# State's part of y in a Mamba and FP4 block: one 64-row float32r contraction for a 16-row float32 one

## The chip, the cores and the metric

The kernel runs on one core of one Trainium2 chip. The metric is the device time of one execution in microseconds, as the median of several runs. The engines have short names in the profile: PE is TensorE (PEld its weight loads), DVE is VectorE, ACT is ScalarE, POOL is GpSimd and SP is SyncE, which here only issues DMA transfers.

## What is computed

One layer of a simplified Mamba block on 8 sequences of 2048 tokens, followed by a gated feed-forward part whose operands are rounded to FP4 by blocks of 16. Everything is float32. Cut to what matters here:

```python
D_MODEL, D_STATE, D_CONV, D_INNER = (256, 16, 4, 512)
xz = x @ W_in
x_proj, z = jnp.split(xz, 2, axis=-1)
x_conv = silu((conv(x_proj) + conv_b))
ssm = x_conv @ W_xproj
delta = jax.nn.softplus(ssm[..., 0])
Bm = ssm[..., 1:1 + D_STATE]
Cm = ssm[..., 1 + D_STATE:]
deltaB = delta[..., None] * Bm
h_mean = jnp.einsum('bld,bln->bdn', x_conv, deltaB) / L
y = jnp.einsum('bdn,bln->bld', h_mean, Cm)
y = y + D[None, None, :] * x_conv
y = y * silu(z)
return y @ W_out
```

`h_mean` is a mean over all tokens of a sequence, so `y` of a sequence's first token needs its last one. The contraction that this case is about is the second einsum: for each token, 512 channels out of 16 states.

## The kernel before

The tokens are worked through in 32 blocks of 512 (four blocks to a sequence), and the second half of the work in pairs of 128-token tiles (two pairs to a block). The program is a list of small pieces. Each piece is entered by `at` with a due time from a hand-written table (`BLOCK` and `PAIR` in the middle, `FIRST`, `BEGIN`, `END`, `FINAL`, `LAST` at the ends, all in us on a plan of 64 us a block), the list is sorted by due time, and the pieces are issued in that order. Every engine runs its own instructions strictly in that order and waits on semaphores for its operands. So a due time sets no clock time: it sets what stands ahead of what in each engine's queue, the SP's DMA queue included.

A block's first part (`begin_block`) loads x transposed, projects it (L756), convolves it (`first` L770 and `tap` L776 on ACT and DVE), applies silu, and then `x_projection` (L802) gives Bm and Cm: one PSUM tile of 128 partitions, four groups of 32 rows, one group to each of four sets of 128 tokens; in a group the first 16 rows are Cm and the last 16 are Bm. `keep_ssm` (L812, ACT) copies it to SBUF as `ct`, in the pool `keep` with six buffers, since Cm is used four blocks later (`LAG` = 4); `by_token` (L817, DVE) transposes it. `weigh` and `softplus` (L651 to L675, with one POOL step `sp_e`, L654) give delta, and `sums` (L896) adds up the state over a sequence in one PSUM bank.

At a sequence's last block, `mean` (L906, ACT) scales that sum, `spread_mean` (L910, TensorE) multiplies it with `spread`, a matrix of ones and zeros that adds the four groups' parts and puts the same result into all four groups of 32 rows, and `keep_mean` (L916, ACT) copies it to SBUF as `hT` (states by channels).

`mix_block` comes four blocks later. `state` (L966) forms y for the block: for each of four chunks of 128 channels and each of four token sets t, a product over the 16 rows of group t, into one of four PSUM banks:

```python
g = slice(t * G, t * G + DS)
nc.tensor.matmul(s["y"][t][:, c, :], hT_of[b][g, c * P : (c + 1) * P], s["ct"][g, :], ...)
```

`mix` (L977, DVE) adds each bank to the skip part in SBUF. `finish_pair` then gates it with silu(z) (`gated`, L1031, POOL), multiplies with W_out (`out`, L1038), normalizes, rounds to FP4, and does the gate, up (L1061) and down products (`tails` L1094 and `down` L1105).

The rounding has a detour that matters here (`quantize_turned`): block scales are turned on DVE (L518), written to DRAM by four small transfers (`gather_scales`, `q_rows`, L524), read back repeated over partitions (`spread_scales`, L531, into `xqT` or `hqT`), while the rounded values are transposed by DMA (`turn`, L538, `q_gT`); POOL multiplies the two (L541). All these transfers, the loads of x (L739, L1004 for `xTz`, L1008 for `xt`), the transposes `hwT` (L841) and the stores (L1118) are issued on SP's one queue. PSUM has seven banks in the pool `ps` for all products and one for the state sum.

Of the kernel before, what the change touches and what calls it, by code (L numbers as in the profile page):

```python
# [8 lines left out]
F32 = mybir.dt.float32  # L9
BF16 = mybir.dt.bfloat16  # L10
U16 = mybir.dt.uint16
AF = mybir.ActivationFunctionType
ALU = mybir.AluOpType
AX = mybir.AxisListType
PSUM = bass.MemoryType.PSUM

P = 128
# [23 lines left out]
    "x_projection": 91.66,  # L41
    "keep_ssm": 94.60,
    "by_token": 99.56,
    "negate": 94.19,
    "exp": 95.71,
    "ratio": 104.25,
# [6 lines left out]
    "mean": 127.54,  # L53
    "spread_mean": 127.90,
    "keep_mean": 129.60,
    "state": 70.83,
    "mix": (79.04, 76.36, 71.79, 75.27),
    "weigh": (90.45, 90.69, 90.49, 92.15),
# [54 lines left out]
    "x_projection": 93.30,  # L113
    "keep_ssm": 109.81,
    "by_token": 112.25,
    "negate": 96.50,
    "exp": 106.60,
    "ratio": 107.91,
# [6 lines left out]
    "mean": 126.28,  # L125
    "spread_mean": 129.37,
    "keep_mean": 130.82,
    "state": 72.50,
    "mix": (74.93, 78.14, 76.66, 78.28),
    "weigh": (85.52, 89.72, 94.26, 90.27),  # L130
# [145 lines left out]
def mamba_fp4_ffn_kernel(  # L276
# [16 lines left out]
    nc = tc.nc  # L293
    B, L, DM = x.shape
    DI = w_out.shape[0]
    DS = (w_xproj.shape[1] - 1) // 2
# [5 lines left out]
    TT = T // P  # L302
# [7 lines left out]
    G = 32  # L310
# [6 lines left out]
    const = ctx.enter_context(tc.tile_pool(name="const", bufs=1))  # L317
    ps = ctx.enter_context(tc.tile_pool(name="ps", bufs=7, space=PSUM))
    ps_h = ctx.enter_context(tc.tile_pool(name="ps_h", bufs=1, space=PSUM))
    dram = ctx.enter_context(tc.tile_pool(name="dram", bufs=2, space=bass.MemoryType.DRAM))  # L320

    ident = const.tile([P, P], F32, name="ident")
# [29 lines left out]
    for dB in dB_of:  # L352
        nc.gpsimd.memset(dB, 0.0)

    place = const.tile([P, G], F32, name="place")
    nc.vector.tensor_reduce(place, ident.rearrange("p (j n) -> p n j", n=G), AX.X, ALU.add)
    spread = const.tile([P, TT, G], F32, name="spread")
    nc.vector.tensor_copy(spread, place.unsqueeze(1).to_broadcast([P, TT, G]))

    xpool = ctx.enter_context(tc.tile_pool(name="xpool", bufs=2))  # L360
    keep = ctx.enter_context(tc.tile_pool(name="keep", bufs=LAG + 2))
    p2 = ctx.enter_context(tc.tile_pool(name="p2", bufs=2))
# [36 lines left out]
    def at(base, table, name, index, f, *args):  # L399
        place = table[name]  # L400
        for i in index:
            place = place[i]
        events.append((base + place, len(events), f, args))

    def bank():
        return ps.tile([P, 512], F32, tag="ps", name="ps")
# [4 lines left out]
    def round_fp4(at_piece, v, n, homes=None, turned=None):  # L411
# [56 lines left out]
        def magnify():  # L468
            nc.scalar.activation(state["g"], state["x"], AF.Abs, scale=GRID)  # L469

# [213 lines left out]
    def layernorm(at_piece, r, nt=NT):  # L684
# [22 lines left out]
        def apply(t):  # L707
            nc.scalar.activation(  # L708
                r()[:, t, :],
                r()[:, t, :],  # L710
                AF.Identity,
                bias=v["nb"][:, t : t + 1],
# [9 lines left out]
    hsum_of, hs_of, hT_of = {}, {}, {}  # L722

    def begin_block(n):
# [5 lines left out]
        b, i = divmod(n, NBLK)  # L730
        early = n < NBLK
        s = tiles["block", n] = {}

        def at_piece(name, f, *args):
            at(n * PERIOD, FIRST if early else BLOCK, name, args, f, *args)
# [31 lines left out]
        def first(c):  # L767
            if "xc" not in s:
                s["xc"] = keep.tile([P, NC, T], F32, tag="xc", name="xc")
            nc.scalar.activation(  # L770
                s["xc"][:, c, :], s["xp", c][:, 0:T], AF.Copy, scale=cw_sb[:, c, 0:1]
            )
# [18 lines left out]
        def silu(c):  # L791
            if "xc" not in s:
                s["xc"] = keep.tile([P, NC, T], F32, tag="xc", name="xc")
            acc = s["xc"][:, c, :]
            nc.scalar.activation(acc, s.pop(("mm", c), acc), AF.Silu, bias=cb_sb[:, c : c + 1])

# [11 lines left out]
                    )  # L808

        def keep_ssm():  # L810
            s["ct"] = keep.tile([P, P], F32, tag="ct", name="ct")
            nc.scalar.copy(s["ct"], s.pop("mm"))  # L812

        def by_token():

# [16 lines left out]
        def split(c):  # L832

            s["hw", c] = p2.tile([P, 2, T], U16, tag="hw", name="hw")
            nc.scalar.copy(
                s["hw", c], s["xc"][:, c, :].bitcast(U16).rearrange("p (n h) -> p h n", h=2)
            )

        def turn(c):
            s["hwT", c] = p2.tile([P, 2, TT, P], U16, tag="hwT", name="hwT")  # L840
            nc.sync.dma_start_transpose(  # L841
                s["hwT", c].rearrange("p h t n -> p (h t) n"),
                s.pop(("hw", c)).rearrange("p h n -> p (h n)"),
            )

        def turned(c):
            if "xct" not in s:
                s["xct"] = p2.tile([P, TT, DI], F32, tag="xct", name="xct", bufs=1)
            nc.scalar.copy(
                s["xct"][:, :, c * P : (c + 1) * P]  # L850
                .bitcast(U16)
                .rearrange("p t (n h) -> p t n h", h=2),
# [51 lines left out]
        def mean():  # L904
            hs = hs_of[b] = p2.tile([P, DI], F32, tag="hs", name="hs", bufs=1)
            nc.scalar.activation(hs, hsum_of.pop(b), AF.Copy, scale=1.0 / L)  # L906

# [4 lines left out]
            )  # L912

        def keep_mean():
            hT_of[b] = p2.tile([P, DI], F32, tag="hT", name="hT", bufs=1)
            nc.scalar.copy(hT_of[b], hs_of.pop("mm"))  # L916

        def skip(c):
            nc.scalar.activation(
                s["xc"][:, c, :], s["xc"][:, c, :], AF.Copy, scale=dk_sb[:, c : c + 1]  # L920
            )

        at_piece("load", load)
        for c in range(NC):
# [10 lines left out]
            at_piece("skip", skip, c)  # L935
        at_piece("x_projection", x_projection)
        at_piece("keep_ssm", keep_ssm)
        at_piece("by_token", by_token)
        for t in range(TT if early else 0):
            at_piece("turn", turn_early, t)  # L940
            at_piece("turned", turned_early, t)
# [9 lines left out]
        if i == NBLK - 1:  # L951
            at_piece("mean", mean)
            at_piece("spread_mean", spread_mean)
            at_piece("keep_mean", keep_mean)

    def mix_block(n):

        b = n // NBLK
        s = tiles["block", n]

        def state():
            s["y"] = [bank().rearrange("p (c n) -> p c n", n=P) for _ in range(TT)]
            for c in range(NC):
                for t in range(TT):
                    g = slice(t * G, t * G + DS)
                    nc.tensor.matmul(  # L966
                        s["y"][t][:, c, :],
                        hT_of[b][g, c * P : (c + 1) * P],
                        s["ct"][g, :],
                        start=True,  # L970
                        stop=True,
                    )

        def mix(g):
            xc = s["xc"].rearrange("p c (t g r) -> p g c t r", g=TT, r=G)[:, g]
            y = s["y"][g].rearrange("p c (t r) -> p c t r", r=G)
            nc.vector.tensor_tensor(xc, xc, y, ALU.add)  # L977

        table = FIRST if n < NBLK else FINAL if n == B * NBLK - 1 else BLOCK
        at((n + LAG) * PERIOD, table, "state", (), state)  # L980
        for t in range(TT):
            at((n + LAG) * PERIOD, table, "mix", (t,), mix, t)
# [312 lines left out]
    for n in range(B * NBLK):  # L1295
        begin_block(n)
        mix_block(n)
        for half in range(T // U):
            finish_pair(n * (T // U) + half)
# [58 lines left out]
```

## Time and profile before

| | |
|---|---|
| Three runs | 1780.77, 1781.19, 1781.21 us (median 1781.19) |
| Span of the profiled execution, first to last instruction | 1781.8 us |
| Granted TensorE clock, mean | 0.995 |
| TensorE busy, 0 to 100 us / 100 to 300 / 300 to 1500 / 1500 to 1782 | 86.2 / 199.0 / 1199.8 / 269.1 us |
| DVE busy in the same four stretches | 77.2 / 182.9 / 1111.8 / 228.1 us |
| State contraction, L966 | 1024 records of matmul, 1024 of weight load |
| DMA packets, and what they moved | 367467, 199.41 MB |

A float32 product is two records in the profile, each with its own weight load. Busy time counts from the first to the last record of overlapping ones; a matmul's end is modelled. The chain that ended last is followed back from the last instruction; in it a group's time runs from its start to the start of what follows. In the lists of groups the columns are: line, engine, operation, output<-inputs, shape, count | busy us, mean ns of one | idle us of the engine before them, and what ended most of it. In a timeline: start us, length us, engine, line, operation, and in brackets the idle time before it and what released it. SPq is SP's DMA queue.

### The profile page before, as it was taken

To read this page: it belongs to the slowest core of one execution; us is meant where nothing else is said; L and a number is where in the kernel's file an instruction comes from. 1 tells how busy PE (TensorE), PEld (TensorE's weight loads), DVE (VectorE), ACT (ScalarE), POOL (GpSimd) and SP (SyncE) were. 2 spreads that over 40 slices of the span, in tenths; PEclk is the share of its full clock that TensorE was granted. 3 is DMA by queue.
4 is the path that set the end of the run, shared out by engine and by line. 5 is a ranking of instruction groups with operands and counts; after the bars stand their busy time and mean duration, and the time that the engine had idled before them with its cause. 6 is when DMAs were issued, how large, how long until landed. Compare 5 with 4: busy or idle time off the path is not lost.

```text
span 1781.8 us, 27851 instructions
## 1 busy us (share of the span) xinstructions
PE 1754.2 (98%) x9646; PEld 1385.7 (78%) x9646; DVE 1600.0 (90%) x3138; ACT 998.7 (56%) x1534; POOL 775.3 (44%) x966
## 2 busy tenths in 40 slices
PE   7999999999999999999999999999999999999997
PEld 3567787787787787787777787777787778888885
DVE  6998999999999999999999989989999989987876
ACT  5786566655566655565655566655566655532232
POOL 2233454444445344444444444344444444544553
PEclk9999999999999999999999999999999999999998
DMA  3234555555556545556544565554555554544432
GB/s 108 71 86 105 125 131 117 113 107 117 120 122 133 114 96 116 122 125 126 116 104 111 122 126 123 116 107 111 122 126 117 121 103 108 117 104 105 113 79 68
DMA packets 367467, 199.41 MB, mean 112 GB/s; under 512 B 290272, under 2 KB 342368, under 8 KB 367328
## 3 DMA queue, kind: packets, MB, share of 16 engines
q1 hardware_dynamic: 367328, 197.65, 49.9%
q8 instruction: 76, 1.25, 0.3%
q14 instruction: 63, 0.52, 0.1%
HBM read 116.34 MB, written 20.91 MB: 77 GB/s over the span
## 4 chain that ended last, share of the span: by engine, by line
PE 94%; DVE 4%; issue 1%; POOL 0%; ACT 0%; DMA 0%; SPq 0%; ACTq 0%; POOLq 0%; DVEq 0%
PE ps L1061 33%; PE ps L1105 15%; PE ps L1015 13%; PE ps L1038 12%; PE ps L756 12%; PE ps L1094 2%; PE ps L966 2%; PE ps L802 2%; PE hsum L896 2%; DVE xc L776 1%; DVE q_amax L438 0%; PE ps L910 0%; PE ps L865 0%; DVE xd L882 0%; DVE q_w L477 0%
## 5 line engine op out<-in xcount | busy, mean ns | idle before, releaser
L1061 PE MATMUL ps<-wgT,xqT 128*128 128x256 f32 (+1 forms) x1512 | 324.4, 361 | 0.0
L1061 PE MATMUL ps<-wuT,xqT 128*128 128x256 f32 (+1 forms) x1512 | 319.6, 361 | 0.0
L1061 PEld LDWEIGHTS ps<-wgT,xqT 128*128 128x128 f32 x1512 | 276.7, 190 | 40.8 <-issue 12.7
L1061 PEld LDWEIGHTS ps<-wuT,xqT 128*128 128x128 f32 x1512 | 275.6, 190 | 38.4 <-issue 12.2
L776 DVE SCALAR_TENSOR_TENSOR xc<-xp,cw_sb,xc 128x512 f32<-128x512 f32 x372 | 282.1, 780 | 13.5 <-DMA dk_sb<-in_L_attn_D_dram 6.3
L541 POOL TENSOR_TENSOR hqT<-q_gT,hqT 128x1408 f32<-128x1408 bf16 x63 | 188.9, 2998 | 230.1 <-DMA q_gT<-q_w 213.9
L1105 PE MATMUL ps<-wdT,hqT 128*128 128x256 f32 x1260 | 288.8, 384 | 0.0
L1079 ACT ACTIVATE sg<-ps 128x512 f32<-128x512 f32 (+1 forms) x189 | 105.4, 558 | 308.4 <-PE ps L1061 260.6
L1031 POOL TENSOR_TENSOR xc<-xc,sz 128x512 f32<-128x512 f32 x128 | 168.5, 1337 | 249.7 <-DVE xc L977 215.7
L1105 PEld LDWEIGHTS ps<-wdT,hqT 128*128 128x128 f32 x1260 | 234.2, 190 | 44.3 <-issue 11.6
L756 PE MATMUL ps<-xT,w_in_sb 128*128 128x512 f32 x512 | 242.1, 598 | 7.0 <-DMA xT<-in_x_t_dram 7.0
L1015 PE MATMUL ps<-xTz,w_in_sb 128*128 128x256 f32 x1024 | 244.3, 382 | 0.0
L1015 PEld LDWEIGHTS ps<-xTz,w_in_sb 128*128 128x128 f32 x1024 | 191.3, 190 | 58.8 <-issue 14.0
L1038 PE MATMUL ps<-w_out_sb,xc 128*128 128x256 f32 x1008 | 228.3, 379 | 0.9 <-POOL xc L1031 0.9
L1038 PEld LDWEIGHTS ps<-w_out_sb,xc 128*128 128x128 f32 x1008 | 190.4, 190 | 37.2 <-issue 11.2
L1026 ACT ACTIVATE sz<-ps 128x512 f32<-128x512 f32 x128 | 75.8, 593 | 245.8 <-PE ps L1015 245.8
L477 DVE SCALAR_TENSOR_TENSOR q_w<-q_w,q_x 128x512 bf16<-128x512 bf16 (+3 forms) x131 | 184.0, 1404 | 2.3
L541 POOL TENSOR_TENSOR xqT<-q_gT,xqT 128x512 f32<-128x512 bf16 x63 | 77.8, 1235 | 228.4 <-DMA xqT<-q_rows 105.8
L708 ACT ACTIVATE x<-x,ln_nb,ln_rs 128x256 f32<-128x256 f32 x256 | 142.3, 591 | 50.2 <-POOL ln_nb L705 42.1
L473 DVE SCALAR_TENSOR_TENSOR q_x<-q_w,q_x 128x512 f32<-128x512 bf16 (+3 forms) x131 | 155.6, 1188 | 14.0 <-ACT q_w L469 13.9
L1086 DVE TENSOR_TENSOR h<-sg,ps 128x512 f32<-128x512 f32 (+1 forms) x189 | 115.3, 631 | 52.8 <-PE ps L1061 48.0
L756 PEld LDWEIGHTS ps<-xT,w_in_sb 128*128 128x128 f32 x512 | 96.4, 192 | 79.7 <-issue 74.8
(128 smaller groups left out, 2440.1 us busy)
## 6 DMA issues: line engine op xcount, KB each, us to landing
hqT<-q_rows SPq DMA_DIRECT2D x63, 704.0 KB
xT<-in_x_t_dram SPq DMA_DIRECT2D x32, 512.0 KB
xTz<-in_x_t_dram SPq DMA_DIRECT2D x64, 256.0 KB
xt<-in_L_attn_x_dram SPq DMA_DIRECT2D x64, 256.0 KB
xqT<-q_rows SPq DMA_DIRECT2D x63, 256.0 KB
out_dram<-x SPq DMA_DIRECT2D x63, 256.0 KB
q_rows<-q_scT SPq DMA_DIRECT2D x252, 4.0 KB
q_rows<-q_scT SPq DMA_DIRECT2D x252, 12.0 KB
```

The lines of the kernel that those rows point to most:

```text
L473: nc.vector.scalar_tensor_tensor(xn, w, 1.5 * GRID, xn, ALU.max, ALU.subtract)
L477: nc.vector.scalar_tensor_tensor(w, w, 1.5 * GRID, xn, ALU.max, ALU.subtract)
L541: nc.gpsimd.tensor_tensor(qT(), state["gT"], qT(), ALU.mult)
L708: nc.scalar.activation(r()[:, t, :], r()[:, t, :], AF.Identity, bias=v["nb"][:, t : t + 1], scale=v["rstd"][:, t : t + 1],)
L756: nc.tensor.matmul(mm, w_in_sb[:, k, c * P : (c + 1) * P], s["xT"][:, k, :], start=(k == 0), stop=(k == KM - 1),)
L776: nc.vector.scalar_tensor_tensor(acc, xp[:, k + 1 : k + 1 + T], cw_sb[:, c, k + 1 : k + 2], acc, ALU.mult, ALU.add)
L1015: nc.tensor.matmul(q["mm", j][:, a, :], w_in_sb[:, k, DI + c * P : DI + (c + 1) * P], q["xT"][:, k, :], start=(k == 0), stop=(k == KM - 1),)
L1031: nc.gpsimd.tensor_tensor(xc, xc, q["sz"][:, c, :], ALU.mult)
L1038: nc.tensor.matmul(mm[:, t, :], s["xc"][:, c, o : o + P], w_out_sb[:, c, :], start=(c == 0), stop=(c == NC - 1),)
L1061: nc.tensor.matmul(q[name, j][:, t, :n], q["xqT"][:, t * KM + k, :], wT[:, k, f0 : f0 + n], start=(k == 0), stop=(k == KM - 1),)
L1086: nc.vector.tensor_tensor(h, q.pop(("sg", j)), up, ALU.mult)
L1105: nc.tensor.matmul(q["d"][t], q["hqT"][:, t * (NF + 1) + j, :], wdT[t][:, t + j, :], start=False, stop=(j == NF - 1),)
```

## The change

The result of `x_projection` is taken apart into a float32r value (`high`, what remains when it is written as float32r) and the exact rest (`low`); the same is done with the state. All four products of the parts then stand under each other on 64 partitions, in one float32r contraction. `cs` has, for each half of 64 partitions (two token sets, side by side in its second dimension), 32 rows of the high part of Cm and 32 of the low part, each twice 16 rows; `hT` alternates high and low by 16 rows. `cs` is made by a detour through DRAM: one write of both parts (`put_parts`) and eight reads (`get_parts`) of 16 partitions each. `hT` is made in two steps: ACT writes the float32r copy, and DVE then forms copy x (0 or -1) + value, so that rows 16 to 31 of each group become the rest. `spread` now repeats the state every 16 rows.

```diff
+    "high": 95.50,
+    "low": 99.60,
+    "put_parts": 101.0,
+    "get_parts": 113.0,
...
+    "part_mean": 129.61,
...
-    place = const.tile([P, G], F32, name="place")
-    nc.vector.tensor_reduce(place, ident.rearrange("p (j n) -> p n j", n=G), AX.X, ALU.add)
-    spread = const.tile([P, TT, G], F32, name="spread")
-    nc.vector.tensor_copy(spread, place.unsqueeze(1).to_broadcast([P, TT, G]))
+    place = const.tile([P, DS], F32, name="place")
+    nc.vector.tensor_reduce(place, ident.rearrange("p (j n) -> p n j", n=DS), AX.X, ALU.add)
+    spread = const.tile([P, P // DS, DS], F32, name="spread")
+    nc.vector.tensor_copy(spread, place.unsqueeze(1).to_broadcast([P, P // DS, DS]))
+
+    low_rows = const.tile([P, 1], F32, name="low_rows")
+    nc.vector.tensor_reduce(
+        low_rows, ident.rearrange("p (j n) -> p n j", n=G)[:, DS:, :], AX.XY, ALU.add
+    )
+    nc.vector.tensor_scalar(low_rows, low_rows, -1.0, None, ALU.mult)
...
         def keep_ssm():
-            s["ct"] = keep.tile([P, P], F32, tag="ct", name="ct")
-            nc.scalar.copy(s["ct"], s.pop("mm"))
+            s["ct"] = p2.tile([P, P], F32, tag="ct", name="ct")
+            nc.scalar.copy(s["ct"], s["mm"])
+
+        def high():
+            s["hl"] = p2.tile([P, 2, P], F32, tag="hl", name="hl")
+            nc.scalar.copy(s["hl"][:, 0, :].bitcast(F32R), s.pop("mm"))
+
+        def low():
+            nc.gpsimd.tensor_tensor(s["hl"][:, 1, :], s["ct"], s["hl"][:, 0, :], ALU.subtract)
+
+        def put_parts():
+            s["parts"] = dram.tile([2, P, P], F32, tag="parts", name="parts")
+            nc.sync.dma_start(s["parts"].rearrange("h p t -> p h t"), s.pop("hl"))
+
+        def get_parts():
+            s["cs"] = keep.tile([P, 2, P], F32, tag="cs", name="cs")
+            for half in range(2):
+                for h in range(2):
+                    o = (half * 2 + h) * G
+                    rows = s["parts"][h].rearrange("(g r) t -> r g t", r=G)
+                    rows = rows[:DS, 2 * half : 2 * half + 2, :]
+                    for rep in range(2):
+                        nc.sync.dma_start(s["cs"][o + rep * DS : o + (rep + 1) * DS], rows)
...
         def keep_mean():
+            hs_of["high"] = p2.tile([P, DI], F32, tag="hs", name="h_high", bufs=1)
+            nc.scalar.copy(hs_of["high"].bitcast(F32R), hs_of["mm"])
+
+        def part_mean():
             hT_of[b] = p2.tile([P, DI], F32, tag="hT", name="hT", bufs=1)
-            nc.scalar.copy(hT_of[b], hs_of.pop("mm"))
+            nc.vector.scalar_tensor_tensor(
+                hT_of[b].bitcast(F32R),
+                hs_of.pop("high"),
+                low_rows,
+                hs_of.pop("mm"),
+                ALU.mult,
+                ALU.add,
+            )
...
             for c in range(NC):
-                for t in range(TT):
-                    g = slice(t * G, t * G + DS)
-                    nc.tensor.matmul(
-                        s["y"][t][:, c, :],
-                        hT_of[b][g, c * P : (c + 1) * P],
-                        s["ct"][g, :],
-                        start=True,
-                        stop=True,
-                    )
+                for j in range(2):
+                    for half in range(2):
+                        g = slice(half * 2 * G, (half + 1) * 2 * G)
+                        nc.tensor.matmul(
+                            s["y"][2 * half + j][:, c, :],
+                            hT_of[b][g, c * P : (c + 1) * P].bitcast(F32R),
+                            s["cs"][g, j, :].bitcast(F32R),
+                            start=True,
+                            stop=True,
+                        )
...
-    nc = _bacc.Bacc("TRN2", target_bir_lowering=False, num_devices=1)
+    nc = _bacc.Bacc(
+        "TRN2", target_bir_lowering=False, num_devices=1, dynamic_dma_scratch_size=1024
+    )
```

All other due times are as they were. In the order that results, on each engine: ACT does `high` right after `keep_ssm`; POOL does `low` after `sp_e` and the gating of a half (two L1031) in an ordinary block; SP has `put_parts` between an `xTz` load and the four `q_rows` transfers, and the eight `get_parts` after the next `xTz` load, just ahead of a `q_gT` transpose; DVE has `part_mean` ahead of some of the convolution's taps.

More of the change, by code (lines that the diff above doesn't have):

```diff
@@ L11 @@
 U16 = mybir.dt.uint16
+F32R = mybir.dt.float32r
 AF = mybir.ActivationFunctionType
@@ L115 @@
     "by_token": 112.25,
+    "high": 109.83,
+    "low": 112.00,
+    "put_parts": 113.0,
+    "get_parts": 123.0,
     "negate": 96.50,
@@ L127 @@
     "keep_mean": 130.82,
+    "part_mean": 130.83,
     "state": 72.50,
@@ L938, in begin_block @@
         at_piece("by_token", by_token)
+        at_piece("high", high)
+        at_piece("low", low)
+        at_piece("put_parts", put_parts)
+        at_piece("get_parts", get_parts)
         for t in range(TT if early else 0):
@@ L954, in begin_block @@
             at_piece("keep_mean", keep_mean)
+            at_piece("part_mean", part_mean)
     def mix_block(n):
```

## Prediction

> **What bounds the kernel now.** I read the busy shares first, then the chain that ended last, then the groups of the state contraction kept apart by shape, then timelines around one batch end and one ordinary block.
>
> ```profile
> PE 1754.2 (98%) x9646; PEld 1385.7 (78%) x9646; DVE 1600.0 (90%) x3138; ACT 998.7 (56%) x1534; POOL 775.3 (44%) x966
> PE 94%; DVE 4%; issue 1%; POOL 0%; ACT 0%; DMA 0%; SPq 0%; ACTq 0%; POOLq 0%; DVEq 0%
> ```
>
> TensorE is the bound: between 300 and 1500 us it is busy for 1199.8 of 1200 us. A microsecond taken from it comes off the end, and one for which it must wait is added. The state contraction and its nearest relatives:
>
> ```profile
> L966 PE MATMUL ps<-ct,hT 16*128 16x128 f32 x1024 | 37.5, 283 | 0.3
> L966 PEld LDWEIGHTS ps<-ct,hT 16*128 16x128 f32 x1024 | 31.4, 186 | 11.3 <-DVE xc L776 3.6 <-ACT hT L916 3.4 <-issue 3.3
> L802 PEld LDWEIGHTS ps<-xc,w_xp_sb 128*32 128x32 f32 x1024 | 26.3, 110 | 11.2 <-issue 7.1 <-DVE xd L882 2.0 <-DVE xc L776 1.0
> L865 PEld LDWEIGHTS ps<-ident,xc 128*128 128x128 f32 x64 | 8.3, 155 | 5.9 <-ACT xc L795 4.6 <-issue 1.3
> ```
>
> One block's state is 16 products in 32 records. In the chain of waits it takes 1.10 us (1.17 where it waited for hT first):
>
> ```profile
> 704.18 0.86 PE ps L910 x2
> 705.03 0.63 PE ps L1094 x4
> 705.71 1.17 PE ps L966 x32
> 729.52 1.01 PE ps L802 x32
> ```
>
> Here a batch ends: spread_mean (L910), a tails group, then state, which starts 0.05 us after hT's copy (705.07 + 0.59) ends. In all eight batches state waits for that copy.
>
> ```profile
> 703.92 4.41 DVE L776 SCALAR_TENSOR_TENSOR xc<-xp,cw_sb,xc 128x512 f32<-128x512 f32 x6
> 705.07 0.59 ACT L916 COPY hT<-ps 128x512 f32<-128x512 f32 x1 [1.22 <-PE ps L910]
> ```
>
> The SP queue of one block, and what it feeds on POOL and TensorE:
>
> ```profile
> 731.01 1.76 SPq L524 DMA_DIRECT2D q_rows<-q_scT  x4
> 734.04 0.62 SPq L531 DMA_DIRECT2D hqT<-q_rows  x1
> 745.89 1.42 SPq L538 DMA_TRANSPOSE q_gT<-q_w  x1
> 735.73 2.50 POOL L1031 TENSOR_TENSOR xc<-xc,sz 128x512 f32<-128x512 f32 x2
> 749.57 2.89 POOL L541 TENSOR_TENSOR hqT<-q_gT,hqT 128x1408 f32<-128x1408 bf16 x1 [6.07 <-DMA q_gT<-q_w]
> 758.44 0.63 PE ps L1094 x4
> ```
>
> hqT is scaled by 752.46, and the tails that read it start at 758.44: six microseconds to spare.
>
> **The contraction itself: -1.6 us.** The build of the changed program has 9134 matmul records where the page shows 9646: 16 fewer in each of 32 blocks, so a product is one record, not two. Four row tiles with 8 records each become two row tiles with 8 each. [...] The weight loads do not fall: loads of 32 columns take 110 ns, of 128 columns 186, whatever the rows; 76 ns for 96 columns, so 101 ns for 128, and eight in a row tile are 0.81 us. [...] I take 1.05, the row with the same load.
>
> [...]
>
> **The wait at a batch's end: +6.1.** hT now needs a copy on ACT (high, as before) and then part_mean on DVE. DVE operations of 128x512 take 0.63 (three mixes in 1.88) to 0.78 us (L776); I take 0.70, plus 0.06 for one more hand-over: 0.76, eight times. Nothing covers it, since state waits for that copy today. It stands in DVE's order behind the two ln_mv pairs of the boundary, at 703.92 in the block shown, so DVE waits there for the copy until 705.67, and the six taps and the mixes behind come 2.4 us later. DVE idles 2.22 us at 717.5 for a product's L1061, which takes most of that up.
>
> **In the first batch the taps behind it are on the path: +2.4.** There DVE does seven taps from 91.70 to 96.92 and mixes at 97.73; POOL gates at 100.36 and TensorE takes L1038 at 101.68 with idle time ahead of it. Now two taps end at 93.2, part_mean runs 96.5 to 97.2, five taps (0.745 each) end at 100.9, and the mixes start 3.2 later, 0.76 of it counted already.
>
> **The detour through DRAM: +8.4.** Each block adds a copy on ACT (0.25 like ct's 0.27; ACT then idles 5.96 us), a subtraction on POOL (128x512 takes 1.25: 0.31, with fixed cost 0.35) and nine transfers on SP at 0.42 to 0.47. None of these is on TensorE's chain; were the covers gone they would cost 8, 11 and 120 us. But they stand in queues. POOL does low after the gated pair, at 738.2 to 738.6. put_parts waits for it and stands before q_rows, which today issue at 731.01. In the changed order's waits there is a second thing: SP's transfers take eight completion semaphores in turn, and the seventh get has the one of hqT, so it waits until hqT (704 KB; its last packet ends 7.2 us after the issue's end, median of 63) has landed; q_gT stands behind. From low: put 0.47, q_rows 1.76, landing 1.27 (732.77 to 734.04), hqT 0.62 + 7.2, two gets 0.85, q_gT 1.42, its landing 2.26 (747.31 to 749.57), POOL 2.89: 18.8 us. In this block 738.6 + 18.8 = 757.4 against 758.4: 1.0 left of six. I did that sum for blocks 6 to 31: twelve have 0.8 to 1.3 left, twelve 1.8 to 3.8, and the last two are late: low at 1487.7 against tails at 1505.65 (0.85 late) and 1536.6 against 1552.93 (2.5 late). That is +3.4. The first pair has the same with xqT: put at 116.6, q_rows to 118.9, xqT 120.1 to 120.8, xTz and eight gets to 124.6, q_gT 3.1 later than its 121.49, and L1061 at 125.5 has 0.1 in hand: +3.0. For inner blocks in which DVE's lateness at a batch end eats the last microsecond I take +2.0 (2.4 late, of which 1.0 to 1.4 is covered, in some two of seven batch ends). Bounds of the chain: 2 us shorter leaves only +1.0 (part of the first pair); 2 us longer puts TensorE about 1 us late in twelve blocks and 2 more in each of the last two, +16. The extra traffic, 0.25 MB in each block or 8 MB to 199 MB, runs beside it.
>
> [...] Row first: L1105 with 20 records takes 4.51 us after a tiled group against 20 x 0.2156 = 4.31. [...]
>
> **Sum:** -1.6 + 6.1 + 2.4 + 8.4 = +15.3. The profiled span is 1781.8, 0.6 above the median of 1781.19; from the median, 1796.5. I say 1797.
>
> **Rivals.**
> [...]
> *The detour is longer*: hqT shares its engines with 16 KB gets and a late xTz, one more microsecond or two, and twelve blocks stall: 1796.5 + 16 - 2 (the inner blocks' share, in it already) = 1811. For: slack of 1.0 in half of the blocks. Against: DMA was idle from 743 to 746.
> [...]
>
> **Chances.** The sum with its own bounds (1789 to 1804, the fourth case in it) 0.52; longer detour 0.22; dearer product 0.06; loads that do not bind 0.20, in it 0.08 faster by over 0.2%, 0.05 within, 0.07 slower. 0.2%, 3.6 us, is about what a measurement here can tell from no change. So faster 0.08, same 0.05, slower 0.87. Range: from 1784, where the third of the fast cases begins, to 1819, which takes in the longer detour and leaves the dearer product out.
>
> **What would show it.** State at 1.05 in the chain with 16 loads still at 186 ns; below 0.80 my first term is wrong. TensorE idle about 0.8 us before each of eight states with DVE as releaser. q_gT issued some 4 us later in a block, POOL's hqT ending within 1.5 us of the tails, and TensorE waiting for POOL's hqT at the tails of the last two blocks; if inner blocks wait too, the detour was under-sized. An unchanged idle table with a shorter state would make the whole forecast wrong.

## The result, and the profile after

The changed kernel takes 1858.22 us (median of 1845.06 to 1860.20) against 1781.20: a ratio of 1.041, with an interval of 1.0376 to 1.0443. The forecast was 1797 with a range from 1784 to 1819; slower was right, the size was not: +77 us instead of +15.3. The profiled execution has a span of 1857.4 us, 75.6 more than before.

From the page of the changed kernel, the busy times and the chain that ended last:

```profile
PE 1775.8 (96%) x9134; PEld 1399.0 (75%) x9134; DVE 1626.5 (88%) x3148; ACT 1006.2 (54%) x1566; POOL 826.8 (45%) x998
PE 65%; DVE 23%; DMA 5%; issue 4%; POOL 1%; ACT 1%; SPq 1%; DVEq 0%; ACTq 0%; POOLq 0%
```

TensorE was 94% of the chain and is 65% now; DVE went from 4% to 23%, DMA from 0 to 5%. TensorE's busy time grew by 21.6 us, so 54.0 of the 75.6 us are idle time: 31.1 of them lie between 300 and 1500 us, where before it idled 0.2. The busy time grew although the contraction has fewer records, because ahead of TensorE's last product the granted clock stood at half for 58.0 us in 13 stretches, against 13.7 us in 3 before. At the batch end shown below, 3.4 us of half clock cost down 1.69 us (6.20 against 4.51), half of them; at that rate it is at most 22.2 us more.

The change moved the lines: the gate and up products L1061 are now L1118, tails L1151 (before L1094), down L1162 (L1105), residual1 L1105 (L1048), POOL's scaling L558 (L541), the normalization of 1408 elements on DVE L478 (L461). The kernels of the experiments differ from that by a few lines again.

The groups of the new operations (the columns are those of before):

```profile
L1023 PE MATMUL ps<-cs,hT 64*128 64x128 f32 x512 | 40.7, 301 | 15.3 <-issue 10.4 <-DVE hT L960 4.9
L1023 PEld LDWEIGHTS ps<-cs,hT 64*128 64x128 f32 x512 | 36.2, 203 | 20.4 <-issue 18.3 <-PE ps L653 1.1
L960 DVE SCALAR_TENSOR_TENSOR hT<-h_high,low_rows,ps 128x512 fp32r<-128x512 f32 x8 | 5.8, 720 | 2.2 <-ACT h_high L956 2.2
```

There are 512 records instead of 1024, as forecast, and part_mean takes 0.72 us (forecast 0.70). The mean of 203 ns a load includes stretches at half clock. But the state's records had 11.3 us of idle time ahead of their loads before and have 20.4 now. The batch end that the prediction showed now stands at 732 in the chain:

```profile
732.19 0.86 PE ps L950 x2
733.05 0.63 PE ps L1151 x4
733.68 2.07 issue
735.75 1.11 PE ps L1023 x16
736.86 6.20 PE ps L1162 x20
743.06 4.75 PE ps L1118 x24
```

State waits 2.07 us, not 0.76, since part_mean starts only at 734.94, behind work for which DVE is itself late. And down (L1162, 20 records) takes 6.20 us instead of 4.51. TensorE by stretches there (busy, granted clock, DMA share, GB/s) tells why:

```profile
735.70:737.20 1.50, 1.45 (x18) 1.00 0.63 120
737.20:739.20 2.00, 2.00 (x7) 0.55 0.27 51
739.20:741.20 2.00, 2.00 (x7) 0.59 0.57 108
741.20:743.20 2.00, 2.00 (x11) 1.00 0.75 189
```

After the idle time the clock is granted at half for 3.4 us.

What makes DVE late shows in the list of waits (engine, line, what was waited for: us in total, times, longest):

```profile
POOL hqT L558 <- DMA q_gT<-q_w: 328.7, 30, 13.8
DVE x L1105 <- DMA out_dram<-x: 68.6, 24, 4.7
PE ps L1118 <- DVE xc L1034: 14.9, 15, 1.5
PE ps L1151 <- POOL hqT L558: 14.7, 10, 3.8
```

The second line has no counterpart before: residual1 (L1105) waits for a store. Here is the SP queue of the next block, and what the eight gets wait for in all blocks:

```profile
769.94 0.36 SPq L842 DMA_DIRECT2D parts<-hl  x1
770.40 1.83 SPq L541 DMA_DIRECT2D q_rows<-q_scT  x4
773.79 0.62 SPq L548 DMA_DIRECT2D hqT<-q_rows  x1
775.04 8.88 SPq L852 DMA_DIRECT2D cs<-parts  x8
784.02 1.43 SPq L555 DMA_TRANSPOSE q_gT<-q_w  x1
785.55 0.71 SPq L1175 DMA_DIRECT2D out_dram<-x  x1
SPq L852 <- DMA hqT<-q_rows: 125.5, 26, 5.2
```

The eight gets take 8.88 us, because the seventh waits for hqT's semaphore; that and their place ahead of q_gT were foreseen. Behind q_gT, though, stands the store, at 785.55. It sends x1 out, of which there are four buffers, and residual1 of a later pair has to wait until its buffer has been sent. Before, the store was issued 5.9 us ahead of residual1:

```profile
748.07 0.38 SPq L1118 DMA_DIRECT2D out_dram<-x  x1
753.94 0.63 DVE L1048 TENSOR_TENSOR x<-xt,ps 128x512 f32<-128x512 f32 x1
754.48 1.61 DVE L461 TENSOR_TENSOR q_x<-h,q_rs 128x1408 f32<-128x1408 f32 x1
```

Here is what DVE and POOL do now:

```profile
787.72 2.88 POOL L558 TENSOR_TENSOR hqT<-q_gT,hqT 128x1408 f32<-128x1408 bf16 x1 [12.34 <-DMA q_gT<-q_w]
788.22 0.69 DVE L1105 TENSOR_TENSOR x<-xt,ps 128x512 f32<-128x512 f32 x1 [3.12 <-DMA out_dram<-x]
788.82 3.26 DVE L478 TENSOR_TENSOR q_x<-h,q_rs 128x1408 f32<-128x1408 f32 x1
790.65 0.70 PE L1151 MATMUL ps<-wdT,hqT 64*128 64x256 f32 x4 [0.55 <-POOL hqT L558]
```

DVE idles 3.12 us until the store has landed. By then POOL has started the scaling of hqT, since q_gT, issued just ahead of the store, has landed too. And the next DVE operation, L478, takes 3.26 us where it takes 1.62 alone: it ends 1.48 us after POOL's. Its groups, before and now:

```profile
L461 DVE TENSOR_TENSOR q_x<-h,q_rs 128x1408 f32<-128x1408 f32 x63 | 105.9, 1680 | 0.0
L478 DVE TENSOR_TENSOR q_x<-h,q_rs 128x1408 f32<-128x1408 f32 x63 | 156.0, 2476 | 0.0
```

That is 50 us more in all. In 25 of 63 pairs it takes over 3 us, each time under POOL's scaling of hqT, which makes 40 us; most of the rest is in 14 pairs in which it starts under the shorter scaling of xqT and takes 2.4 to 2.6. The tails (L1151) wait only 0.55 us for POOL: what the prediction watched is a small part of it.

### The profile page after: what moved, and what is told of

It is laid out like the page before. It is cut to its first block, busy times and chain, and to the rows that moved or that the text cites. A ratio compares the mean times of both kernels' runs of the same rounds, so it can differ in the third digit from the quotient of the medians.

```text
span 1857.4 us, 27357 instructions
## 1 busy us (share of the span) xinstructions
PE 1775.8 (96%) x9134; PEld 1399.0 (75%) x9134; DVE 1626.5 (88%) x3148; ACT 1006.2 (54%) x1566; POOL 826.8 (45%) x998
## 4 chain that ended last, share of the span: by engine, by line
PE 65%; DVE 23%; DMA 5%; issue 4%; POOL 1%; ACT 1%; SPq 1%; DVEq 0%; ACTq 0%; POOLq 0%
PE ps L1118 26%; PE ps L1162 11%; PE ps L773 8%; PE ps L1095 8%; PE ps L1072 7%; DVE xc L793 6%; DVE q_x L478 4%; DMA out_dram<-x 3%; DVE q_amax L455 2%; DVE h L1143 2%; PE ps L1151 1%; PE ps L819 1%; DVE ln_st L711 1%; DVE q_x L490 1%; DVE q_w L494 1%
## 5 line engine op out<-in xcount | busy, mean ns | idle before, releaser
L1118 PE MATMUL ps<-wgT,xqT 128*128 128x256 f32 (+1 forms) x1512 | 328.6, 363 | 14.9 <-DVE xc L1034 14.9
L558 POOL TENSOR_TENSOR hqT<-q_gT,hqT 128x1408 f32<-128x1408 bf16 x63 | 181.8, 2886 | 358.1 <-DMA q_gT<-q_w 328.7
L1118 PE MATMUL ps<-wuT,xqT 128*128 128x256 f32 (+1 forms) x1512 | 323.5, 364 | 3.4 <-POOL xqT L558 3.4
L1118 PEld LDWEIGHTS ps<-wgT,xqT 128*128 128x128 f32 x1512 | 275.4, 190 | 61.1 <-DVE xc L1034 21.5
L1118 PEld LDWEIGHTS ps<-wuT,xqT 128*128 128x128 f32 x1512 | 275.3, 191 | 46.1 <-issue 12.2
L1162 PE MATMUL ps<-wdT,hqT 128*128 128x256 f32 x1260 | 305.0, 400 | 0.0
L793 DVE SCALAR_TENSOR_TENSOR xc<-xp,cw_sb,xc 128x512 f32<-128x512 f32 x372 | 289.9, 801 | 11.1 <-ACT xc L787 7.8
L1162 PEld LDWEIGHTS ps<-wdT,hqT 128*128 128x128 f32 x1260 | 245.8, 199 | 47.8 <-issue 11.6
L486 ACT ACTIVATE q_w<-q_x 128x512 bf16<-128x512 f32 (+3 forms) x131 | 130.3, 994 | 83.8 <-DVE q_x L478 79.7
L490 DVE SCALAR_TENSOR_TENSOR q_x<-q_w,q_x 128x512 f32<-128x512 bf16 (+3 forms) x131 | 149.9, 1144 | 11.6 <-ACT q_w L486 11.2
L478 DVE TENSOR_TENSOR q_x<-h,q_rs 128x1408 f32<-128x1408 f32 x63 | 156.0, 2476 | 0.0
L889 ACT COPY xct<-hwT 128x1024 uint16<-128x1024 uint16 x112 | 129.1, 1160 | 44.5 <-DMA hwT<-hw 43.8
```

Of the source, the lines that this page charges most:

```text
L478: nc.vector.tensor_tensor(x, by_block(v()), rs.unsqueeze(len(rs.shape)).to_broadcast(x.shape), ALU.mult,)
L490: nc.vector.scalar_tensor_tensor(xn, w, 1.5 * GRID, xn, ALU.max, ALU.subtract)
L558: nc.gpsimd.tensor_tensor(qT(), state["gT"], qT(), ALU.mult)
L793: nc.vector.scalar_tensor_tensor(acc, xp[:, k + 1 : k + 1 + T], cw_sb[:, c, k + 1 : k + 2], acc, ALU.mult, ALU.add)
L1118: nc.tensor.matmul(q[name, j][:, t, :n], q["xqT"][:, t * KM + k, :], wT[:, k, f0 : f0 + n], start=(k == 0), stop=(k == KM - 1),)
L1162: nc.tensor.matmul(q["d"][t], q["hqT"][:, t * (NF + 1) + j, :], wdT[t][:, t + j, :], start=False, stop=(j == NF - 1),)
```

## Experiments

**The change in its three parts.** Each of the first three kernels keeps the contraction and leaves out the detour, part_mean or both; the fourth is complete and moves the detour.

`a1_contraction`: the contraction alone.

```diff
-                            s["cs"][g, j, :].bitcast(F32R),
+                            cs_fixed[g, j, :].bitcast(F32R),
...
-        at_piece("high", high)
-        at_piece("low", low)
-        at_piece("put_parts", put_parts)
-        at_piece("get_parts", get_parts)
...
-            nc.scalar.copy(hs_of["high"].bitcast(F32R), hs_of["mm"])
+            nc.scalar.copy(hT_of[b].bitcast(F32R), hs_of.pop("mm"))
...
-            at_piece("part_mean", part_mean)
```

> The float32r contraction alone: neither the detour nor part_mean; the state reads a fixed tile of zeros in place of C's parts, and hT is the plain copy, so State's part of y is left out. As forecast (loads bind, nothing else changes): state 1.05, -1.6 us, 1779.6. Other theory, from the changed kernel's trace, where the time from the first tails record to the record behind state is 1.475 us against 1.736 before (tails and state now follow each other 0.28 us closer, state itself 0.02 longer): 28 blocks x 0.26 and three x 0.06, -7.5, 1773.7.

Measured 1776.45 us (1776.05 to 1776.67), ratio 0.9969 (0.9957 to 0.9982): -4.75. The chain of this kernel:

```profile
756.33 0.63 PE ps L1148 x4
756.96 0.84 PE ps L1020 x16
757.80 4.51 PE ps L1159 x20
```

and its loads:

```profile
L1020 PEld LDWEIGHTS ps<-cs_fixed,hT 64*128 64x128 f32 x512 | 32.8, 188 | 5.3 <-ACT hT L958 3.4 <-issue 1.0
```

A float32r load takes 188 ns, as a float32 one does (186). Tails and state together take 1.47 us, against 0.63 + 1.10 = 1.73. By the records' starts the 0.26 lie at the seam: the first state record stands 0.35 us behind the first of the tails, where it stood 0.63 behind, and state itself is no shorter.

`a2_mean`: the contraction and part_mean; of the edits above, those on `cs` and the detour alone.

> The contraction with part_mean on DVE, without the detour (State reads the fixed zeros, its part of y is left out). As forecast for the wait at batch ends and the first taps: +6.1 and +2.4 on top of the contraction alone, so 1782 if that is 1773.7. Rival (the wait and the halved clock behind it are part_mean's own doing): at seven batch ends the changed kernel's trace has 1.4 to 3.6 us more ahead of L1162 and 1.7 lost to a granted clock of 0.5: about 4 us eight times, 1805. If the detour makes DVE late and so the wait long, there is no clock of 0.5 at batch ends here.

Measured 1791.23 us (1786.01 to 1792.13), ratio 1.0044 (1.0028 to 1.0060), 14.8 above the contraction alone; the profiled execution was the shortest, 9.5 above. A batch end in its chain:

```profile
707.52 0.87 PE ps L952 x2
708.42 0.59 ACT h_high L958
709.04 0.76 DVE hT L962
709.93 1.11 PE ps L1021 x16
711.04 4.51 PE ps L1160 x20
```

This is the wait as forecast: TensorE idles 0.92 us at six batch ends and 2.38 at the last, and down stays at 4.51. The 2 us waits of the changed kernel are not part_mean's own. The other executions, some 5 us longer, had a mean granted clock of 0.993 instead of 0.998; they have no trace. In the traced one none of TensorE's idle times of 2.4 to 2.9 us past 100 us was followed by a half clock; whether some were in the others is not shown.

`a3_detour`: the contraction and the detour; of the edits above, those on the mean alone.

> The contraction with the detour, without part_mean: hT is the plain rounded copy, so the low half of the state's mean is left out. As forecast: +8.4 on top of the contraction alone, 1782 if that is 1773.7. Theory now (put and gets at their place on SP hold q_gT and the store behind them, so hqT and x1's buffers are late in every block): most of the 85 us between 1773.7 and 1858 is here, 1825 to 1850. Rival (part_mean's wait and the clock are the larger part): under 1805.

Measured 1833.25 us (1828.64 to 1839.01), ratio 1.0287 (1.0264 to 1.0310), 56.8 above the contraction alone. From its list of waits:

```profile
DVE x L1104 <- DMA out_dram<-x: 67.2, 27, 4.1
```

So the wait for the store needs no part_mean. The parts give 14.8 + 56.8; together they cost 81.8 more than the contraction alone, 10 more than their sum.

`a4_later`: complete.

```diff
-    "put_parts": 101.0,
-    "get_parts": 113.0,
+    "put_parts": 110.0,
+    "get_parts": 121.5,
```

> Complete; only two due times differ from the changed kernel: put_parts from 101 to 110 (behind the scales' gathers and hqT's issue), get_parts from 113 to 121.5 (behind q_gT and the store). If the place on SP is what costs: near the contraction with part_mean alone, 1780 to 1790, q_gT issued some 4 us earlier in the block than in the changed kernel and no wait of DVE's residual1 for the store above 1 us. If the traffic and the eight issues cost wherever they stand: 1840 to 1860. If part_mean is the larger part: 1805 to 1825.

Measured 1795.18 us (1791.66 to 1796.85), ratio 1.0069 (1.0054 to 1.0084). Two due times take 63 us off, with the same traffic and the same issues: it is the place. 4 us remain above the kernel with part_mean.

**Which link of the detour.** The next four change one link each.

`b1_x1`:

```diff
-            q["x1"] = keep.tile([P, NT, DM], F32, tag="x1", name="x1", bufs=4)
+            q["x1"] = keep.tile([P, NT, DM], F32, tag="x1", name="x1", bufs=5)
```

> The changed kernel with five buffers for x1 instead of four; complete. Theory: the store stands on SP behind the gets, x1's buffer comes free late, and DVE's residual1 waits for it with all of DVE's queue behind it (68.6 us in 24 waits in the changed kernel); with a fifth buffer that wait is gone: 1795 to 1815. Rival: TensorE is late because hqT is late, and DVE's wait only fills time that TensorE would lose anyway: 1840 to 1860, with longer waits of the tails for POOL's hqT.

`b2_put`:

```diff
-    "put_parts": 101.0,
+    "put_parts": 110.0,
```

> The changed kernel with put_parts alone moved from 101 to 110, so that the scales' gathers and hqT's issue no longer stand behind its wait for POOL's low; the gets stay ahead of q_gT and the store. If put's wait is the root (189.4 us in 26 waits on SP): hqT is issued some 4 us earlier, the seventh get hardly waits for it, 1795 to 1810. If eight gets ahead of q_gT and the store are the root: 1830 to 1858.

`b3_get`:

```diff
-    "get_parts": 113.0,
+    "get_parts": 121.5,
```

> The changed kernel with get_parts alone moved from 113 to 121.5, behind q_gT and the store; put_parts stays ahead of the scales' gathers. If the gets are the root (8.8 us on SP between hqT and q_gT): 1795 to 1810 and no wait of DVE for the store. If put's wait is the root: 1830 to 1858.

| kernel | us | ratio to before |
|---|---|---|
| `b1_x1` | 1807.04 (1806.21 to 1813.29) | 1.0146 (1.0127 to 1.0166) |
| `b2_put` | 1804.13 (1801.56 to 1806.70) | 1.0121 (1.0107 to 1.0135) |
| `b3_get` | 1801.55 (1798.67 to 1802.29) | 1.0104 (1.0090 to 1.0117) |

Each was meant to tell a root from a consequence, and each alone takes off 51 to 57 us. So there is no single root, but a chain of which every link is needed for the full loss. `b1_x1` is the telling one: its SP queue is as late as in the changed kernel (the gets wait 126.6 us for hqT, against 125.5), but DVE no longer waits for the store, and L478's mean falls to 1864 ns.

```profile
SPq L852 <- DMA hqT<-q_rows: 126.6, 26, 5.4
L478 DVE TENSOR_TENSOR q_x<-h,q_rs 128x1408 f32<-128x1408 f32 x63 | 117.4, 1864 | 0.0
```

`d1_swap` asks whether it is the wait for the store or the collision behind it.

```diff
 PAIR = {
-    "residual1": (100.47, 123.55),
+    "residual1": (100.47, 125.10),
```

> The changed kernel with one due time moved: residual1 of a pair's second half from 123.55 to 125.10, so that on DVE the normalization L478 of 1408 elements stands ahead of residual1 instead of behind it; the SP queue and x1's four buffers stay. In the changed kernel DVE is released by the store just after POOL has begun L558, and L478, next on DVE, then ends only some 1.5 us after POOL's L558 has ended: 3.2 us instead of 1.62 in 25 pairs, 54 us over all 63 above 1.62. If this collision carries the loss: the excess falls under 20 us, the wait for the store loses most of its sum too since the blocks no longer get later, 1800 to 1820. If the wait for the store is enough by itself: it stays above 50 us, and the time above 1835.

Measured 1809.28 us (1808.12 to 1811.09), ratio 1.0154 (1.0141 to 1.0168): 49 us off with a swap of two neighbours on DVE, the queue and the buffers as they were. Its wait for the store, in the list of waits:

```profile
DVE x L1105 <- DMA out_dram<-x: 22.2, 23, 2.3
```

and L478 among its groups:

```profile
L478 DVE TENSOR_TENSOR q_x<-h,q_rs 128x1408 f32<-128x1408 f32 x63 | 121.5, 1929 | 1.0
```

There are still 23 waits, of 1 us instead of 2.9, and L478 never starts under the scaling of hqT. So the swap does two things at once: L478 fills a part of the wait, and it no longer meets POOL. How much of the 49 us each brings it does not separate, nor do the other kernels: L478 starts under that scaling 26 times in the changed kernel, 26 in `a3_detour`, 8 in `b3_get` and never in the other kernels of the table, and the wait for the store is 68.6, 67.2 and 5.0 us there, 22.2 here, 1.6 in `a4_later` and nothing in the rest. The blocks get later and later only where both are large. How much later, all kernels show in one table: the start of x_projection in some blocks (counted from 0), in us later than before, with block 0 set equal:

```
block            4     5     8    12    16    20    24    28    31
changed        4.2  10.0  14.0  24.1  32.0  39.5  47.2  56.1  68.0
a1_contraction -0.2  0.2  -0.2  -1.1  -1.9  -2.8  -3.6  -4.5  -5.2
a2_mean        2.9   3.2   3.6   3.7   3.7   3.7   3.8   3.8   3.0
a3_detour      0.0   5.9   8.8  14.9  21.0  25.2  27.3  32.0  43.6
a4_later       5.0   5.7   7.0   7.1   7.2   7.3   7.4   7.5   6.7
b1_x1          4.3  11.9  14.4  15.6  16.9  17.7  18.3  19.0  21.3
b2_put         4.3  12.0  12.5  12.6  12.7  12.8  12.9  13.0  13.4
b3_get         5.0   6.5   8.8   8.9   8.9   8.9   8.9   8.9   8.7
d1_swap        3.3   7.4  10.6  12.2  12.2  12.7  12.7  13.9  18.5
```

The changed kernel loses some 8 us in every batch to the end; with one link cut, it is 9 to 14 us late by block 8 and loses 0.1 to 4.6 in the next 20 blocks. The forecast's detour was of the second kind. That the loss feeds itself (late DVE, late mixes and gating, late low on POOL, late put, late store, late DVE) is how I read this; the runs show only that each cut stops it.

**Hiding part_mean.** `b4_behind` adds to `a4_later`:

```diff
-    "part_mean": 129.61,
+    "part_mean": 133.6,
...
-    "part_mean": 130.83,
+    "part_mean": 135.9,
...
-        at((n + LAG) * PERIOD, table, "state", (), state)
+        late = 2.2 if n % NBLK == 0 and table is BLOCK else 0.0
+        at((n + LAG) * PERIOD + late, table, "state", (), state)
```

with the mixes later by the same 2.2.

> Complete: put_parts and get_parts as in the kernel with both moved; part_mean behind the six taps that stand behind it on DVE (seven taps' order in the first batch), and, at the seven batch ends after the first, state behind down, so that 20 records of down cover part_mean. If part_mean's wait is what is left: 14.8 us (1791.2 less 1776.45) less the first batch's share of about 4, so some 10 less than 1795: 1783 to 1788. If the later mixes then hold DVE (they start some 4 us later at a batch end): 1790 to 1797.

Measured 1788.96 us (1788.24 to 1790.23), ratio 1.0036 (1.0024 to 1.0049). In seven blocks the last mix comes behind the gating of the first pair here, so that a part of State's y is added ungated. `c1_behind2` shifts only the mix that stood ahead of state, and by less.

```diff
-            at((n + LAG) * PERIOD + late, table, "mix", (t,), mix, t)
+            at((n + LAG) * PERIOD + late * 0.6 * (t == 2), table, "mix", (t,), mix, t)
```

> Complete. Both moved as before (110, 121.5), part_mean behind the taps, state behind down at seven batch ends, but of the mixes only the one that stood ahead of state is moved, so all four stand ahead of the gating. The waits of 1.2, 1.0 and 1.2 us that the last attempt had at 1578 to 1591 came with its later mixes: 1784 to 1787 if they go, 1788 to 1790 if part_mean's place costs there by itself.

Measured 1783.67 us (1781.34 to 1785.95), ratio 1.0007 (0.9999 to 1.0016). `c2_best` adds another place of the detour for blocks 4 to 7 and of part_mean in the first batch.

```diff
-    "part_mean": 135.9,
+    "part_mean": 133.2,
...
-        at_piece("put_parts", put_parts)
-        at_piece("get_parts", get_parts)
+        for k, (name, f) in enumerate((("put_parts", put_parts), ("get_parts", get_parts))):
+            at(n * PERIOD + (4.1, 19.5)[k] * (n // NBLK == 1), FIRST if early else BLOCK, name, (), f)
```

> Complete; c1_behind2 with part_mean one tap earlier in the first batch, and for blocks 4 to 7 put_parts behind q_gT (114.1) and get_parts at 141, since the kernel with both moved lost 2.5 us on part_mean alone between blocks 3 and 8. If that is the detour's place in the first pairs: 1782 to 1785, level with before at best. If it is POOL's or DVE's work: as c1_behind2.

Measured 1782.06 us (1780.11 to 1784.59), ratio 0.9998 (0.9989 to 1.0007). It cannot be told from the kernel before: what the contraction brings, the first batch takes (its block 5 is 2.8 us late, block 31 then 1.9 early).

**Where the contraction's gain comes from.** `c3_down` is `a1_contraction` with state behind down, and the mix that stood ahead of it moved as in `c1_behind2`.

```diff
-        at((n + LAG) * PERIOD, table, "state", (), state)
+        late = 2.2 if table is BLOCK else 0.0
+        at((n + LAG) * PERIOD + late, table, "state", (), state)
```

> a1_contraction (State's part of y left out) with state behind down instead of behind tails in blocks 4 to 30. If the 0.26 us a block come from state's 64-row tiles following tails' 64-row tiles: gone, three changes of tiling a block as before, and 1781 to 1782, the x_projections' starts no earlier than before. If they come from the float32r product itself (half the records, loads as long): still 1776 to 1777.

Measured 1788.83 us (1784.39 to 1789.74), ratio 1.0032 (1.0020 to 1.0045). Its chain:

```profile
760.54 0.63 PE ps L1148 x4
761.17 4.51 PE ps L1159 x20
765.69 1.04 PE ps L1020 x16
766.73 4.95 PE ps L1115 x24
```

State is 1.04 here and the 24 records behind it 4.95, where `a1_contraction` has 0.84 and 4.75. Its blocks get 0.11 us later each (block 12 starts 0.5 late, block 28 2.2), where that kernel's get 0.2 earlier (1.1 and 4.5 early). So the gain is the seam between tails and state, both on 64 rows, and hardly the product. The expectation counted as many changes of tiling as before. But tails, down, state and the gate products now alternate between 64 and 128 rows, which makes four changes where the kernel before has three and `a1_contraction` two; from tails to the end of those 24 records the chain takes 11.13 us here and 10.73 there, 0.2 for each of the two more. The total is 7 us more than expected. Of the 6.0 us by which the profiled execution is longer than that of the kernel before, 1.2 lie ahead of the first x_projection, 2.6 between the first and the last and 2.2 behind it; the first and the third are not explained.

## Why the prediction was wrong, step by step

- **The contraction itself** (-1.6 forecast, -4.75 measured). The reasoning on loads held: float32r loads take 188 ns in `a1_contraction`, float32 ones 186 before. The 0.05 us a block behind the 1.6, though, are a term that no run shows. What the runs show is that, behind the first ones, the records of a row tile of state follow each other every 0.112 us, before and in the changed kernel alike, and a state of 1.04 us in `c3_down`, behind down, against 1.10 before, behind the tails. What failed is the price of the seam between tails and state: the forecast gave it nothing. Tails took 0.63 us before state and before L1105 alike, but in the kernel before both were changes of tiling, so these rows could not tell it. The runs can: on 64 rows state follows the tails 0.28 us closer, and the two more changes in `c3_down` cost 0.2 us each, what L1105 takes behind the tails above 20 records of 0.216 us (4.51 against 4.31).
- **The wait at a batch's end and the first taps** (+6.1 and +2.4). About right in the trace of `a2_mean`: 0.92 us six times, 2.38 once where 0.76 was forecast, and 2.9 us by block 4 where 0.76 and 2.4 were. In the medians it is 14.8, of which the traces show the 9.5 of the profiled executions; the rest stays open.
- **The detour through DRAM** (+8.4 forecast; +56.8 alone, +67 on top of the other two). This is the step that failed. Its chain from low to the tails was the right one, with two errors. The smaller is its length: from the end of low to the end of POOL's scaling the changed kernel takes 20.5 us (median of blocks 6 to 31, 19.8 to 22.2) where the sum had 18.8. In the block shown it takes 20.7 (769.91 to 790.60), and 1.6 of the 1.9 more lie between the issues of hqT and q_gT. The forecast had a price for that, at most +16 for 2 us, and TensorE waited 14.7 us for POOL's hqT at the tails (and 3.4 in the first pair, where 3.0 was forecast). The larger error is that the chain ended at the tails. The sentence "q_gT stands behind" stopped one entry short: behind q_gT stands the store, and who waits for a store was not asked. Before, it was issued 5.9 us ahead of residual1 and took 2.6 to land (785.55 to 788.14 in the changed kernel), so it had an estimated 3.3 us to spare. In the changed kernel it is issued 5.1 us ahead of the tails (785.55 and 790.65), before 10.4 (748.07 and 758.44): 5.3 less. The upper bound for "2 us longer" (+16) was built on the same chain and was too low for the same reason.
- **The rivals.** "The detour is longer" was right in its place and in its microsecond or two, but it priced a wait of the tails. That its 1811 is near what the kernel takes with any one link cut (1801 to 1809) can be chance: in `b1_x1`, where the chain to the tails is as late, they wait only 10.1 us for hqT. The dearer product and the loads that do not bind are both out: 1.04 us for the state, 188 ns for a load.
- **Left out altogether:** that a late DVE operation can meet POOL's, at 1.6 us a time (L478 takes 3.26 us instead of 1.62), and that TensorE's clock can halve after an idle time (2.07 us at the batch end shown), at 1.7 a time (down takes 6.20 us instead of 4.51).

## What to carry to other kernels

When a transfer is put ahead of others in a queue, follow every entry behind it to its reader, stores too: a store's reader is the next writer of its buffer, and the slack is the time from the store's landing to that writer. Price a delay with what the delayed operation will meet, not only with its length; here a swap of two neighbours on DVE, which shortened a wait and avoided such a meeting, took off 49 of 77 us. And where the blocks of a kernel get later and later, try the cheapest cut first: here each of four stopped most of it, and three of them were one due time.

## What the runs showed of the hardware

- **DVE and POOL.** In the changed kernel L478 started 26 times under POOL's L558 on hqT and each time ended 1.48 us after it: 3.1 to 3.5 us instead of 1.62 (1.97 once, when it started late), while POOL's 2.88 stayed. The other way round, as 16 times in `b1_x1`, L478 keeps 1.61 and L558 ends 2.7 to 2.9 us after it. What makes the later one end so late is not shown.
- **The clock.** In all traces, no idle time of TensorE up to 1.55 us was followed by a half clock; of those from 1.67 us, 61 of 85 were (every one in the changed kernel past 100 us, but one of six in `a2_mean`), for 3.4 us or two or three times that. Why the other 24 were not is not shown.
- **The seam.** In the changed kernel state, on 64 rows, follows the tails, also on 64, 0.28 us closer (0.35 us from first record to first record, 28 times) than it did before, on 16 rows (0.63).
